# A modulated-convolution kernel whose T1 operand is summed by a DMA in place instead of by GpSimd, with a second G buffer and T0/T4 made one turn sooner

## The chip, the cores and the metric

The kernel runs on one core of a Trainium2 chip. A core has five engines with a queue of instructions each: PE (TensorE, matrix products; PEld is its weight load), DVE (VectorE), ACT (ScalarE), POOL (GpSimd) and SP (SyncE, which here only issues DMAs). An engine takes its instructions strictly in the order of the program and waits on semaphores. The metric is the device time of one execution in microseconds; lower is better.

## The reference

The input x has 128 images of 64 channels and 1024 positions in float32. Each image goes through four 1-D convolution layers of three taps, whose weights are modulated by a style vector of its own, and the result is added to x:

```python
s = style @ mw.T + mb
weight = SCALE * w * s[:, None, :, None]
demod = lax.rsqrt(jnp.sum(weight * weight, axis=(2, 3)) + EPS)
weight = weight * demod[:, :, None, None]
# 'same':       conv, K=3
# 'upsample':   transposed conv with stride 2, then a blur of 4 taps
# 'downsample': blur of 4 taps, then conv with stride 2
# layers: same, upsample, same, downsample
x = x + layers(x)
```

No layer has a nonlinearity, so the four layers of one image are one linear filter along the position axis.

## The kernel before, in words

The kernel uses that linearity. For each group of four images it builds the weights of one combined filter from the four layers (the chain: scale3, stage1, stage2, stage3), and then applies that filter to x. The filter has nine taps. They are applied by a fast-convolution scheme (three by three taps): x is laid out in three planes (position modulo 3), five combinations T0 to T4 of these planes are formed, each is multiplied with its own combination of weights (the five products m = 0 to 4, each three taps), and sums of the products give the three output planes. There are 32 groups q of four images. Two images lie in the two halves of the 128 partitions and two side by side, so that every product is made of matmuls of 64 by 64 weights and 340 positions.

On the way to T0 to T4 stands G, an intermediate of three planes for each of two image pairs: in_g01 writes its planes 0 and 1 and in_g2 its plane 2, all from X, the loaded input. From G come T1 = plane 2 + plane 1 (in1), T2 = plane 2 - plane 1 (in2), and T0 and T4 together (in04). T3 comes from X (in3).

The order is written out by hand: the program is not rescheduled, and each engine's queue holds its instructions in the order in which the Python code issues them. After five opening turns, turn_of(q) runs for q = 4 to 28, and a written-out end follows. In one turn the stages of several groups are mixed: n = q + 1, c = q + 2, s = q + 4. The turn contains the last products of q (conv2, conv4, conv0), the first of n (conv3, conv1), stage2 and stage3 of the weights of c, and stage1 of s. `entry` is true for q = 4 alone.

The places that the change and the prediction's steps touch:

- POOL in a turn: r_sums (L638, two sums of R, the weights after stage2; they are read by the last of the seven groups of matmuls of stage3_b, L621), in2 (L781), a sum of S (L484), in1 (L776).
- DVE in a turn: sum2 (L712 into Y, read by conv4), a difference (L862), six weight combinations (combine_a, combine_b), in04 (L790), share_sums (L501), in_g2, side work that differs from turn to turn (SIDE), two sums of S (L481), in_g01, sum1 (L712 into y, after conv1), in3 (L761), and in turn 13 two instructions of LATE.
- PE in a turn: stage2 (L506), conv2 (L803), stage3_b (L621), conv4 (L803 into Y), stage3_a, conv3, stage1_a (L428), conv0, stage1_b, share, conv1.
- A helper records many instructions under one line: L712 is sum_of, L399 scaled_copy, L803 product.

G has one buffer before, the T tiles have two each, X has two.

Of the kernel before, what the change touches and what calls it, by code (L numbers as in the profile page):

```python
# [48 lines left out]
F32 = mybir.dt.float32  # L49
AF = mybir.ActivationFunctionType  # L50
ALU = mybir.AluOpType
# [12 lines left out]
def kernel(  # L64
# [10 lines left out]
    NP, P, NXC = x.shape  # L75
    B = 2 * NP
    NQ = B // 4
# [5 lines left out]
    nc_v, nc_a, nc_g = nc.vector, nc.scalar, nc.gpsimd  # L83
# [3 lines left out]
    const = ctx.enter_context(tc.tile_pool(name="const", bufs=1))  # L87
# [4 lines left out]
    wf_pool = ctx.enter_context(tc.tile_pool(name="wf_pool", bufs=3))  # L92
    tpool = ctx.enter_context(tc.tile_pool(name="tpool", bufs=2))
    mpool = ctx.enter_context(tc.tile_pool(name="mpool", bufs=1))
    gpool = ctx.enter_context(tc.tile_pool(name="gpool", bufs=1))
    opool = ctx.enter_context(tc.tile_pool(name="opool", bufs=2))
    ps_conv = ctx.enter_context(tc.tile_pool(name="ps_conv", bufs=2, space=PSUM))
    ps_w = ctx.enter_context(tc.tile_pool(name="ps_w", bufs=1, space=PSUM))
# [39 lines left out]
    PL = NXC // 3  # L138
# [27 lines left out]
    def unit(pool, name):  # L166

        if pool is ps_w:
            return [pool.tile([P, 512], F32, tag=f"u{r}", name=f"{name}_{r}") for r in range(2)]
        t = pool.tile([P, 2, 512], F32, tag="u", name=name)  # L170
        return [t[:, r, :] for r in range(2)]


    NB = 340
# [266 lines left out]
    def flat(t):  # L441
        return t.rearrange("c a o -> c (a o)")
# [92 lines left out]
    def stage2_rest(q):  # L535

        ps = shared_ps.pop(q)
        block = lambda i, n=1: [b[:, i * C : (i + n) * C] for b in ps]
        apart = [b[:, : 4 * C].rearrange("c (a b o) -> c a b o", a=2, b=2)[:, :, 0] for b in ps]
        plan = (  # L540
            (apart, E[:, 0], slice(1, 4, 2)),
            (block(1), Ed[:, 0], slice(2, 3)),
            (block(2), Ed[:, 1], slice(1, 2)),
            (block(3), E[:, 2], slice(3, 4)),
            (block(3), Ed[:, 2], slice(2, 3)),
            (block(4), Ed[:, 3], slice(1, 2)),
            (block(4), E[:, 4], slice(3, 4)),
            (block(5, 2), E[:, 8], slice(2, 4)),
            (block(5), E[:, 6], slice(3, 4)),
            (block(1, 2), E[:, 1], slice(4, 6)),  # L550
            (block(2), E[:, 3], slice(4, 5)),
            (block(3), Ed[:, 4], slice(5, 6)),
            (block(4), Ed[:, 5], slice(4, 5)),
            (block(5), E[:, 7], slice(5, 6)),
        )
        for n, (dst, weight, slots) in enumerate(plan):
            chain_matmul(dst, weight, chain[q], slots, n == len(plan) - 1)
        return ps

    def stage2(q, pool=None, engs=(nc_a, nc_a), between=None):  # L560
        if q in shared_ps:
            ps = stage2_rest(q)
        else:
            ps = opened.pop(q, None)
            taps = range(9) if ps is None else range(3, 9)
            ps = stage2_taps(q, taps, ps or unit(pool or ps_w, f"psR{q}"))
        if between:
# [168 lines left out]
    Ts = {}  # L736
    Gs = {}
# [5 lines left out]
    def plane(buf, i, pairs=BOTH_PAIRS):  # L743

        at = PL * (2 - i) if i < 3 else PL * 2 + 1
        return buf[:, pairs, at : at + NJ]
# [16 lines left out]
    def in_g01(q, pairs=BOTH_PAIRS):  # L763
        if q < NQ:
            X, g = g_tile(q)
            sum_of(g[:, pairs, PL:], X[:, pairs, : 2 * PL], 0.5, X[:, pairs, PL:], ALU.subtract)

    def in_g2(q, pairs=BOTH_PAIRS):
        if q < NQ:
            X, g = g_tile(q)  # L770
            sum_of(plane(g, 2, pairs), plane(X, 3, pairs), 0.5, plane(X, 2, pairs), ALU.subtract)

    def in1(q, eng):
        if q < NQ:
            t, g = t_tile(q, "T12"), Gs[q]
            eng.tensor_add(t[:, :, 0, :NJ], plane(g, 2), plane(g, 1))  # L776

    def in2(q, eng):
        if q < NQ:
            t, g = t_tile(q, "T12"), Gs[q]  # L780
            eng.tensor_sub(t[:, :, 1, :NJ], plane(g, 2), plane(g, 1))  # L781

    def in04(q, pairs=BOTH_PAIRS):
        if q < NQ:
            t, g = t_tile(q, "T04"), Gs[q]
            a, b = g[:, pairs, :NJ], g[:, pairs, 2 * PL : 2 * PL + NJ]
            both = lambda v, step: bass.AP(
                v.tensor, v.offset, [*(list(d) for d in v.ap[:-1]), [step, 2], [1, NJ]]
            )
            nc_v.tensor_sub(t[:, pairs, :, :NJ], both(a, PL), both(b, 1))  # L790

    def product(q, m, ps, groups=range(K), alone=False):

        W, H_ = Wq[q]
        tag, i = SLOT[m]
        for g in groups:
            for s, rows in enumerate(HALF):
                for c, cols in enumerate(HALF):
                    if m in (0, 4):
                        w = W[rows, tap(m // 2, g), c, :]  # L800
                    else:
                        w = H_[rows, m - 1, g, c, :]
                    nc.tensor.matmul(  # L803
                        ps[s][cols, :NB],
                        w,
                        Ts[q, tag][rows, c, i, g : g + NB],
                        start=(g == 0 and (m == 3 or alone)),
                        stop=(g == K - 1),
                        skip_group_check=True,
                    )  # L810
# [36 lines left out]
    def sum1(q):  # L847

        y1w[q] = m_tile("y1", q, 2)
        for s, a in parts(q):  # L850
            sum_of(y1w[q][:, s], a, 2.0, m3c[q][:, s])
# [35 lines left out]
            os[q][:, s, planes].rearrange("c i j -> c (i j)"),  # L887
        )


    raw = const.tile([P, 512], F32, name="raw")

    WIDE = 6
    ends_ps = {}
# [94 lines left out]
    g1 = const.tile([P, 6, C], F32, name="g1")  # L989

    Ye = [const.tile([P, HB, 8], F32, name=f"Ye{s}") for s in range(2)]
    Ue = [const.tile([P, HB, 11], F32, name=f"Ue{s}") for s in range(2)]
    Ve = [const.tile([P, HB, 12], F32, name=f"Ve{s}") for s in range(2)]
    Oe = const.tile([P, B, 3], F32, name="Oe")
# [295 lines left out]
    def small(q):  # L1290
        l, bs = SMALL[q]
        dst = high(bs.stop - bs.start)
        src = c0f if l == 0 else cc[l - 1]
        for cols in HALF:
            nc.tensor.matmul(
                dst[cols], wsum[T, l, :], src[T, bs], start=False, stop=True, skip_group_check=True
            )
# [66 lines left out]
    def side(work, q):  # L1364
        work.get(q, lambda: None)()
# [117 lines left out]
    def turn_of(q):  # L1483
        n, c, s = q + 1, q + 2, q + 4
        entry = q == FIRST
        stage2(c)
        if entry:
            sum2(q)
            conv4(q)
            combine_a(n)  # L1490
            r_sums(c, nc_v)
        else:
            conv2(q)
            r_sums(c, nc_g)
            sum2(q)
            in2(n, nc_g)
        side(TABLES, q)
        for i in range(3):
            load(c + 1, slice(i, i + 1))
        stage3_b(c, open_a(n))  # L1500
        if entry:
            conv0(q, 0, 1)
        else:
            combine_a(n)
            conv4(q)
        stage3_a(c)
        combine_b(n)
        conv3(n)
        if entry:
            copy_m3(n)  # L1510
            stage1_a(s)
        outputs(q, 2)
        if not entry:
            if s < NQ:
                stage1_a(s)
            copy_m3(n)
        in04(n)
        if sharing(q):
            share_sums(c + 1)
        in_g2(c)  # L1520
        side(SIDE, q)
        if q in SMALL:
            l, bs = SMALL[q]
            nc_v.memset(high(bs.stop - bs.start), 0.0)
        conv0(q, *((2,) if entry else range(K)))
        if entry:
            conv1(n, 0, 1)
        outputs(q, 1)
        if s < NQ:
            stage1_b(s)  # L1530
        in_g01(c)
        if sharing(q):
            share(c + 1, banks(q))
            share_copy(c + 1)
        outputs(q, 0)
        if q in SLOTS:
            matmuls, width, rest = SLOTS[q]
            slot(matmuls, width, Y_banks)
            rest()
        if s == NQ:  # L1540
            slot(ends3, 3, unit(ps_w, "psE"), 3)
            rest3()
        conv1(n, *((2,) if entry else range(K)))
        if q in SMALL:
            small(q)
        sum1(n)
        in3(c)
        side(LATE, q)
        if s == NQ:
            in04(c)  # L1550
        in1(c, nc_g)
        if s + 1 < NQ:
            scale3(s + 1)

# [3 lines left out]
        turn_of(q)  # L1558

    q, n, c = NQ - 3, NQ - 2, NQ - 1  # L1560
    stage2(c)
    conv2(q)
    in2(n, nc_g)
    stage3(c, 0)
    sum2(q, (0,))
    combine_a(n)
# [26 lines left out]
    q, n = NQ - 2, NQ - 1  # L1593
# [128 lines left out]
```

## Time and profile before

| | us |
|---|---|
| median of 3 runs | 476.29 (475.52 to 476.63) |
| span of the profiled execution, first to last instruction | 475.5 |
| PE busy | 469.7 |
| DVE busy | 417.3 |
| ACT busy | 312.0 |
| POOL busy | 165.8 |
| one steady turn (201.44 to 215.28) | 13.84 |

For the profiled execution the profile gives the span and no separate time; the lowest of the three runs, 475.52, is the same as this span to the last digit shown, so nothing that can be seen lies around it. The granted TensorE clock is 0.998 over the span.

The profile is to be read as follows. PE's busy time is that of pipelined matmuls, and one row of a group of matmuls overlaps the next by a little, so the distance from one start to the next is the better measure. A float32 matmul of the program shows as two records in the trace (one product of 12 matmuls is x24). "Idle before" is the time that an engine had nothing to run ahead of an instruction, with what released it.

### The profile page before, as it was taken

How to read it: one execution, taken by the hardware profiler on the slowest of the kernel's cores; microseconds unless marked ns; L12 is line 12 of the kernel's file. 1: busy time of each engine (PE TensorE's matmuls, PEld its weight loads, DVE VectorE, ACT ScalarE, POOL GpSimd, SP SyncE). 2: the span in 40 equal slices, each digit the busy share in tenths (PEclk: the TensorE clock that was granted, in tenths of full speed). 3: DMA queues.
4: the chain of work that ended last, by engine and by line, in shares of the span. 5: the costliest groups of instructions: out<-in, count | busy, mean ns of one | idle time of the engine just before them, and what ended most of it. 6: DMA issues, size and time to landing. Idle time of an engine off the chain costs nothing.

```text
span 475.5 us, 26771 instructions
## 1 busy us (share of the span) xinstructions
PE 469.7 (99%) x11932; PEld 349.5 (74%) x11932; DVE 417.3 (88%) x694; ACT 312.0 (66%) x711; POOL 165.8 (35%) x200
## 2 busy tenths in 40 slices
PE   9999999999999999999999999999999999999996
PEld 6987788777678876677776677766788787876653
DVE  3889998879989998899979899979998999999896
ACT  4565657577766676766667666667666777766464
POOL 3634033664444342233432233422333423243200
PEclk9999999999999999999999999999999999999999
DMA  5237456535445554345544454543555544455225
GB/s 176 71 115 224 150 151 180 152 113 177 139 145 166 166 166 136 123 150 169 163 150 126 130 168 152 178 124 121 152 164 169 164 145 147 148 152 161 80 91 193
DMA packets 52707, 70.71 MB, mean 149 GB/s; under 512 B 6000, under 2 KB 50672, under 8 KB 52592
## 3 DMA queue, kind: packets, MB, share of 16 engines
q1 hardware_dynamic: 52368, 68.78, 46.3%
q8 instruction: 93, 1.52, 1.4%
q10 hardware_dynamic: 224, 0.22, 0.1%
q14 instruction: 22, 0.18, 0.1%
HBM read 35.36 MB, written 33.62 MB: 145 GB/s over the span
## 4 chain that ended last, share of the span: by engine, by line
PE 99%; DVE 0%; ACT 0%; issue 0%
PE psA L803 47%; PE Y L803 12%; PE psR L506 9%; PE psW L621 7%; PE psA L621 7%; PE psS L428 6%; PE psR L589 5%; PE psA L506 2%; PE Y L1044 2%; PE Y L183 1%; PE Y L379 1%; PE psM L220 0%; PE psE L1044 0%; PE Y L255 0%; DVE o L882 0%; PE psM L255 0%
## 5 line engine op out<-in xcount | busy, mean ns | idle before, releaser
L803 PE MATMUL psA<-T,H 64*64 64x340 f32 x2304 | 185.9, 446 | 0.0
L803 PEld LDWEIGHTS psA<-T,H 64*64 64x64 f32 x2304 | 90.7, 133 | 46.9 <-issue 2.5
L712 DVE SCALAR_TENSOR_TENSOR G<-X 128x1376 f32<-128x1376 f32 (+2 forms) x65 | 78.0, 1206 | 0.2
L776 POOL TENSOR_TENSOR T<-G 128x684 f32<-128x684 f32 x28 | 46.3, 1652 | 73.7 <-DVE G L712 73.7
L484 POOL TENSOR_TENSOR S<-S 128x128 f32<-128x128 f32 x28 | 21.6, 772 | 139.7 <-ACT S L399 139.6
L399 ACT ACTIVATE R<-psR,tC 128x448 f32<-128x448 f32 x63 | 36.6, 631 | 43.6 <-PE psR L506 25.8
L803 PE MATMUL psA<-T,Wf 64*64 64x340 f32 x768 | 63.7, 446 | 0.0
L803 PE MATMUL Y<-T,Wf 64*64 64x340 f32 x768 | 62.4, 451 | 0.0
L712 DVE SCALAR_TENSOR_TENSOR Y<-m,psA 128x340 f32<-128x340 f32 x62 | 32.0, 516 | 28.2 <-PE psA L803 26.9
L399 ACT ACTIVATE psW<-psA 128x128 f32<-128x128 f32 x100 | 19.3, 268 | 49.1 <-PE psA L621 45.0
L790 DVE TENSOR_TENSOR T<-G 128x1368 f32<-128x1368 f32 (+1 forms) x33 | 50.8, 1541 | 0.0
L399 ACT ACTIVATE Wf<-psW,t 128x256 f32<-128x256 f32 (+2 forms) x76 | 32.7, 480 | 26.7 <-PE psW L621 26.4
L761 DVE TENSOR_TENSOR T<-X 128x684 f32<-128x684 f32 x32 | 47.7, 1492 | 0.0
L506 PE MATMUL psR<-S,E 64*64 64x64 f32 (+1 forms) x1472 | 46.8, 237 | 0.0
L781 POOL TENSOR_TENSOR T<-G 128x684 f32<-128x684 f32 x28 | 46.5, 1660 | 0.0
L428 PEld LDWEIGHTS psS<-wd,w2n 64*64 64x64 f32 x1120 | 35.1, 133 | 12.9 <-issue 0.3
L506 PEld LDWEIGHTS psR<-S,E 64*64 64x64 f32 x1472 | 39.5, 134 | 4.9 <-ACT psR L529 0.2
L803 PEld LDWEIGHTS Y<-T,Wf 64*64 64x64 f32 x768 | 30.3, 132 | 16.8
L803 PEld LDWEIGHTS psA<-T,Wf 64*64 64x64 f32 x768 | 29.8, 133 | 14.5
L880 ACT ACTIVATE o<-psA,tb,td 128x340 f32<-128x340 f32 x63 | 37.1, 648 | 5.0 <-PE psA L803 2.8
L880 ACT ACTIVATE o<-y,tb,td 128x340 f32<-128x340 f32 x62 | 38.5, 678 | 0.0
L880 ACT ACTIVATE o<-Y,tb,td 128x340 f32<-128x340 f32 x62 | 36.1, 639 | 2.8 <-PE Y L803 2.0
(180 smaller groups left out, 840.4 us busy)
## 6 DMA issues: line engine op xcount, KB each, us to landing
out<-o SPq DMA_DIRECT2D x191, 170.0 KB, 2.6
X<-in_x SPq DMA_DIRECT2D x150, 172.0 KB, 3.4
X<-in_x SPq DMA_DIRECT2D x14, 516.0 KB, 5.0
par<-in_params SPq DMA_DIRECT2D x3, 192.0 KB, 3.8
Xe<-in_x_ends SPq DMA_DIRECT2D x1, 512.0 KB, 4.5
out<-Oe SPq DMA_DIRECT2D x2, 96.0 KB, 2.1
out<-o ACTq DMA_DIRECT2D x1, 170.0 KB, 2.8
par<-in_params SPq DMA_DIRECT2D x1, 160.0 KB, 2.7
```

Source lines behind the costliest of these rows:

```text
L399: nc_a.activation(dst, src, AF.Copy, scale=f)
L428: nc.tensor.matmul(ps[r][cols, at * C : (at + n) * C], weight[rows], wd[c if r == 0 else 1 - c][rows, taps], start=first, stop=last, skip_ ...
L506: nc.tensor.matmul(dst[r][cols], weight[rows], st[c if r == 0 else 1 - c][rows, slots, :], start=False, stop=last, skip_group_check=True,)
L589: nc.tensor.matmul(ps[r][cols, lo * C : (lo + m) * C], E[rows, e + 2, :], src[rows, a, :], start=(n == 0), stop=(n == 8), skip_group_check ...
L621: nc.tensor.matmul(dst[r][cols], weight[rows], t[rows, c, slots, :], start=first, stop=last, skip_group_check=True,)
L712: nc_v.scalar_tensor_tensor(out, x, f, y, op0=ALU.mult, op1=op)
L761: nc_v.tensor_sub(t[:, pairs, 0, :NJ], plane(X, 3, pairs), plane(X, 1, pairs))
L776: eng.tensor_add(t[:, :, 0, :NJ], plane(g, 2), plane(g, 1))
L781: eng.tensor_sub(t[:, :, 1, :NJ], plane(g, 2), plane(g, 1))
L790: nc_v.tensor_sub(t[:, pairs, :, :NJ], both(a, PL), both(b, 1))
L803: nc.tensor.matmul(ps[s][cols, :NB], w, Ts[q, tag][rows, c, i, g : g + NB], start=(g == 0 and (m == 3 or alone)), stop=(g == K - 1), skip_ ...
L880: nc_a.activation(dst, src, AF.Identity, bias=add, scale=d3)
```

## The change

T1 is no longer a tile of its own in the steady turns. A DMA issued from POOL's queue adds G's plane 1 onto G's plane 2 in place (in1_dma), and the product m = 1 reads its moving operand from there. Since this overwrites plane 2, T2, T0 and T4 of the same group must be made before: in2 moves from the start of the turn of q = n - 1 to the turn before that, ahead of sum1 in the code, and in04 to the end of that turn, behind in3. Since G now lives until conv1 has read it, G has two buffers. in_g01 follows in_g2 directly, ahead of the side work and of the two sums of S. The scratch tile raw, used in the opening, takes over the place of Ye[0]. The opening turns keep in1 and in2 as they were; the entry turn q = 4 does in04 both for n and for c.

```diff
-    gpool = ctx.enter_context(tc.tile_pool(name="gpool", bufs=1))
+    gpool = ctx.enter_context(tc.tile_pool(name="gpool", bufs=2))
...
+    def in1_dma(q):
+
+        g = Gs[q]
+        nc_g.dma_start(plane(g, 2), plane(g, 1), accum_op=ALU.add)
+        first_of[q] = g[:, :, :PL]
...
     def product(q, m, ps, groups=range(K), alone=False):
...
+        if m == 1 and q in first_of:
+            src = first_of[q]
+        else:
+            src = Ts[q, tag][:, :, i]
...
-                        Ts[q, tag][rows, c, i, g : g + NB],
+                        src[rows, c, g : g + NB],
...
-    raw = const.tile([P, 512], F32, name="raw")
...
+    raw = Ye[0].rearrange("c b e -> c (b e)")
...
     def turn_of(q):
         n, c, s = q + 1, q + 2, q + 4
         entry = q == FIRST
+        if not entry:
+            in1_dma(n)
         stage2(c)
...
             conv2(q)
             r_sums(c, nc_g)
             sum2(q)
-            in2(n, nc_g)
...
-        in04(n)
+        if entry:
+            in04(n)
         if sharing(q):
             share_sums(c + 1)
         in_g2(c)
+        in_g01(c)
         side(SIDE, q)
...
             stage1_b(s)
-        in_g01(c)
...
+        in2(c, nc_g)
         sum1(n)
         in3(c)
         side(LATE, q)
-        if s == NQ:
-            in04(c)
-        in1(c, nc_g)
+        in04(c)
...
     q, n, c = NQ - 3, NQ - 2, NQ - 1
+    in1_dma(n)
     stage2(c)
     conv2(q)
-    in2(n, nc_g)
```

Where instructions stand in a queue, from the built programs. In the names, the number behind a letter is the group q and the one behind the underscore a buffer; what stands in brackets are the queues whose semaphores the instruction waits for.

POOL's queue before, from r_sums of group 14 to the sum of S of group 17 (L638 is r_sums, L781 in2, L776 in1):

```order
L638 TENSOR_TENSOR R14_3858<-R14_3858 128x2x128 [waits Activation_49]
L781 TENSOR_TENSOR T12_13_3796<-G13_3729 128x2x342
L484 TENSOR_TENSOR S16_3991<-S16_3991 128x2x64 [waits Activation_49]
L776 TENSOR_TENSOR T12_14_4066<-G14_3999 128x2x342 [waits DVE_49,PE_49,Pool_49]
L638 TENSOR_TENSOR R15_4128<-R15_4128 128x2x128 [waits Activation_49]
L781 TENSOR_TENSOR T12_14_4066<-G14_3999 128x2x342
L484 TENSOR_TENSOR S17_4261<-S17_4261 128x2x64 [waits Activation_49]
```

And now (L789 is in2, L781 the DMA of in1_dma):

```order
L638 TENSOR_TENSOR R14_3860<-R14_3860 128x2x128 [waits Activation_49]
L484 TENSOR_TENSOR S16_3992<-S16_3992 128x2x64 [waits Activation_49]
L789 TENSOR_TENSOR T12_14_4061<-G14_3998 128x2x342 [waits DVE_49,PE_49]
L781 DMA G14_3998<-G14_3998 128x2x342 [waits DMASW6_49,DVE_49,Pool_49]
L638 TENSOR_TENSOR R15_4130<-R15_4130 128x2x128 [waits Activation_49]
L484 TENSOR_TENSOR S17_4262<-S17_4262 128x2x64 [waits Activation_49]
```

The sum L776 is gone, in2 stands where it stood, and the DMA, which waits for DVE (in04) and for in2, stands directly ahead of r_sums.

DVE's queue before, from the sums of S of group 15 to sum2 of group 12 (L712 into G is in_g01, L761 in3, L712 into Y sum2):

```order
L481 SCALAR_TENSOR_TENSOR S15_3721<-psS15_1_3708,tB_132,S15_3721 128x128 [waits PE_49,Activation_49]
L712 SCALAR_TENSOR_TENSOR G13_3729<-X1_106 128x2x688 [waits DMAHW2_49,DMAHW1_49]
L712 SCALAR_TENSOR_TENSOR y1_12_3792<-psA12_3614,m3_12_3724 128x680 [waits PE_49,Activation_49]
L761 TENSOR_TENSOR T3_13_3794<-X1_106 128x2x342
L712 SCALAR_TENSOR_TENSOR Y_119<-m3_12_3724,psA12_3614 128x340 [waits PE_49]
```

And now (L798 is in04):

```order
L712 SCALAR_TENSOR_TENSOR G13_3728<-X1_106 128x2x688 [waits DMAHW2_49,DMAHW1_49]
L1077 TENSOR_TENSOR Ye0_159<-Ye0_159,c0_155 128x64x6
L481 SCALAR_TENSOR_TENSOR S15_3722<-psS15_0_3708,tB_132,S15_3722 128x128 [waits PE_49,Activation_49]
L481 SCALAR_TENSOR_TENSOR S15_3722<-psS15_1_3709,tB_132,S15_3722 128x128 [waits PE_49,Activation_49]
L712 SCALAR_TENSOR_TENSOR y1_12_3793<-psA12_3615,m3_12_3725 128x680 [waits PE_49,Activation_49]
L761 TENSOR_TENSOR T3_13_3795<-X1_106 128x2x342
L798 TENSOR_TENSOR T04_13_3797<-G13_3728 128x4x342 [waits DVE_49]
L712 SCALAR_TENSOR_TENSOR Y_119<-m3_12_3725,psA12_3615 128x340 [waits PE_49]
```

in_g01 has moved ahead of the side work and the sums of S, and in04 from behind the weight combinations to a place between in3 and sum2.

PE's queue now, where stage3_b of group 15 ends and conv4 begins:

```order
L621 MATMUL psA14_4155<-R15_4130,par_97 64x64 x4
L621 MATMUL psA14_4155<-R15_4130,w0s0_150 64x64 x8
L621 MATMUL psA14_4155<-R15_4130,par_97 64x128 [waits Pool_49]
L621 MATMUL psA14_4155<-R15_4130,par_97 64x128 x3
L815 MATMUL Y_119<-T04_13_3797,Wf13_3616 64x340 [waits DVE_49]
```

The order on PE is what it was; the third row is the one that waits for r_sums.

More of the change, by code (lines that the diff above doesn't have):

```diff
@@ L776, in in1 @@
             eng.tensor_add(t[:, :, 0, :NJ], plane(g, 2), plane(g, 1))
+    def in1_dma(q):
+        g = Gs[q]
+        nc_g.dma_start(plane(g, 2), plane(g, 1), accum_op=ALU.add)
+        first_of[q] = g[:, :, :PL]
+    first_of = {}
     def in2(q, eng):
```

## The prediction

> **What bounds the kernel now.** I read the page's busy table first, then the stages, the waits, and last the timeline of one turn. The page (engine, busy time, share of the span, instructions; then a group of instructions with its idle time; then the one DMA queue with real traffic):
>
> ```profile
> PE 469.7 (99%) x11932; PEld 349.5 (74%) x11932; DVE 417.3 (88%) x694; ACT 312.0 (66%) x711; POOL 165.8 (35%) x200
> L776 POOL TENSOR_TENSOR T<-G 128x684 f32<-128x684 f32 x28 | 46.3, 1652 | 73.7 <-DVE G L712 73.7
> q1 hardware_dynamic: 52368, 68.78, 46.3%
> ```
>
> The span is 475.5 us and PE is busy for 469.7 of them: not more than 5.8 us can be gained anywhere while the matmuls stay as they are. POOL works 35% of the time, and in front of L776, the sum that the change takes off POOL, it sat idle for 73.7 us. Two successive steady turns as stages (length, then busy time of each engine), and the waits of the steady part:
>
> ```profile
> 201.44:215.28 13.84, 13.84 (x392) 9.79 (x388) 12.73 (x20) 9.79 (x24) 4.81 (x4) 1.00 0.49 155
> 215.28:229.12 13.84, 13.84 (x392) 9.79 (x388) 12.69 (x21) 9.68 (x24) 4.81 (x4) 1.00 0.50 157
> 345.93:360.19 14.26, 14.06 (x395) 12.15 (x391) 13.27 (x20) 10.00 (x24) 4.46 (x4) 1.00 0.49 152
> ```
> ```profile
> POOL T L776 <- DVE G L712: 60.0, 22, 3.3
> POOL R L638 <- ACT R L399: 35.1, 23, 3.9
> DVE Y L712 <- PE psA L803: 23.9, 22, 1.9
> ```
>
> A turn is 13.84 us of unbroken PE at full clock; one turn of the others is 14.26. The other engines wait for PE, never the reverse for long. So the change cannot win much; it can only be free, or make PE wait. Whether it does is decided at the start of a turn. The timeline there (start, length, engine, line, shape, and in brackets the idle time before):
>
> ```profile
> 210.03 1.58 DVE L790 TENSOR_TENSOR T<-G 128x1368 f32<-128x1368 f32 x1
> 211.53 0.42 DVE L501 TENSOR_TENSOR S<-S 128x256 f32<-128x256 f32 x1
> 211.86 0.87 DVE L712 SCALAR_TENSOR_TENSOR G<-X 128x684 f32<-128x684 f32 x1
> 212.64 0.81 DVE L1066 TENSOR_TENSOR Ye<-Ye,c 128x384 f32<-128x384 f32 x1
> 213.38 0.60 DVE L481 SCALAR_TENSOR_TENSOR S<-psS,tB,S 128x128 f32<-128x128 f32 x2
> 213.90 1.58 DVE L712 SCALAR_TENSOR_TENSOR G<-X 128x1376 f32<-128x1376 f32 x1
> 215.42 0.87 DVE L712 SCALAR_TENSOR_TENSOR y<-psA,m 128x680 f32<-128x680 f32 x1
> 216.21 1.81 DVE L761 TENSOR_TENSOR T<-X 128x684 f32<-128x684 f32 x1
> 219.00 1.07 DVE L712 SCALAR_TENSOR_TENSOR Y<-m,psA 128x340 f32<-128x340 f32 x2 [0.98 <-PE psA L803]
> ```
> ```profile
> 212.21 0.82 POOL L484 TENSOR_TENSOR S<-S 128x128 f32<-128x128 f32 x1 [5.16 <-ACT S L399]
> 215.64 1.65 POOL L776 TENSOR_TENSOR T<-G 128x684 f32<-128x684 f32 x1 [2.61 <-DVE G L712]
> 218.56 0.72 POOL L638 TENSOR_TENSOR R<-R 128x256 f32<-128x256 f32 x1 [1.27 <-ACT R L399]
> 219.25 1.65 POOL L781 TENSOR_TENSOR T<-G 128x684 f32<-128x684 f32 x1
> ```
> ```profile
> 213.38 1.90 PE L803 MATMUL psA<-T,H 64*64 64x340 f32 x24
> 217.03 1.90 PE L803 MATMUL psA<-T,H 64*64 64x340 f32 x24
> 219.86 0.40 PE L621 MATMUL psA<-R,par 64*64 64x128 f32 x8
> 220.12 1.95 PE L803 MATMUL Y<-T,Wf 64*64 64x340 f32 x24
> 221.88 0.40 PE L621 MATMUL psW<-R,wsq 64*64 64x128 f32 x8
> 227.22 1.90 PE L803 MATMUL psA<-T,H 64*64 64x340 f32 x24
> ```
>
> PE ends conv1 at 215.28 (213.38 + 1.90) and conv2 at 218.93 (217.03 + 1.90). At 219.86 stands the last group of stage3_b, the only one that reads what r_sums (POOL L638) writes; r_sums ends at 219.28. This pair has 0.58 us to spare, and it is what the change touches.
>
> **The change part by part.** PE keeps its instructions and shapes: 0. The second buffer of G, the smaller raw, and T1's new address add no instruction: 0.
>
> POOL loses 24 sums of 1.65 us. They were hidden by POOL's idle time (2.61 us ahead of this one), so that alone is worth 0. The difference (in2) moves ahead of the turn's end. It needs in_g01, which now follows in_g2: DVE comes free of the weight combinations at 210.03, then share_sums, in_g2 and in_g01 take 0.33, 0.78 and 1.52 (starts 211.53 to 211.86 to 212.64, and 213.90 to 215.42), to 212.66. POOL's L484 (0.82 us, which needs ACT at 212.21) ends by 213.5 even if it waits for in_g01, and in2 by 215.2. The conv2 that reads it is that of the next turn but one, at 217.03 + 13.84, more than 15 us later: 0.
>
> DVE's in3 gets shorter. It took 1.81 us beside POOL's in1; nearer the end of the kernel, with POOL at rest, it took less:
>
> ```profile
> 454.29 0.87 DVE L712 SCALAR_TENSOR_TENSOR G<-X 128x684 f32<-128x684 f32 x1
> 455.07 0.87 DVE L761 TENSOR_TENSOR T<-X 128x684 f32<-128x684 f32 x1
> ```
>
> With in2 over by 215.2, in3 should take 0.87, and 0.94 us of DVE time a turn come free. DVE waits for PE next, so this is worth 0 by itself; but it sets when in04 ends. The Trainium skill, SBUF — State Buffer, section Who interferes with whom, says that a DVE instruction with two SBUF inputs and a POOL instruction that reads SBUF exclude each other for the whole instruction; 1.81 against 0.87 agrees (in3 ended 0.73 us after in1 did). Were the 1.81 in3's own, the wait worked out below would be 0.94 us longer in each turn, 22.6 us more.
>
> in04 moves from 210.03 to behind in3. The sum before it (L712, y) can start 0.07 us after conv1, as L712 at 219.00 does after conv2: 215.35. With steps of 0.79 (215.42 to 216.21) and 0.78, in3 starts at 216.14 and in04 at 216.92; in04 ends at 218.50. The next DVE instruction waits for conv2 until 219.00, so DVE is not late.
>
> The DMA is new. POOL issues it after in04 of the same image, at 218.50 + 0.07 = 218.57, and r_sums stands directly behind it in POOL's queue. r_sums would have started at 218.56. So whatever time POOL needs to issue the DMA, call it t, lands on r_sums whole: it starts at 218.57 + t. Of the spare 0.58 us, 0.07 go by until PE sees that r_sums is done (as between conv2's end and 219.00), and 0.01 by the later start. PE waits t - 0.5 us. Nothing gives it back: the wait delays conv1, conv1 delays in3 and in04, and these set the next issue. It is paid in all 24 turns that have r_sums on POOL:
>
> ```profile
> L638 POOL TENSOR_TENSOR R<-R x24: 724/730/897, 105.2 to 432.8; 128x256 f32<-128x256 f32 x24
> L146 SPq DMA_DIRECT2D X<-in_x x164: 327/423/2069, 3.6 to 433.7; - x164
> DMA to landing us min/median/max: 2.3/3.5/6.6
> ```
>
> No row shows a DMA issued by POOL, so t is bounded by SP's issues (ns, minimum, median, maximum). Lower end: 0.33 us, SP's shortest, no wait. Upper end: 2.07, SP's longest: 1.57 x 24 = 37.7 us. I take three times SP's median, 1.27 us. A load of one plane reads 128 runs and writes 128; the accumulation has two runs per partition, reads source and destination and writes, 768 against 256. That it also lies between SP's 0.42 and the 1.65 of the POOL instruction that handles the same planes makes it plausible. It is an estimate. The wait is then 0.77 us, and 24 x 0.77 = 18.5 us.
>
> The Trainium skill, DMA: Bandwidth & Descriptors, section Latency and other measured facts, puts a POOL-issued DMA's first byte at about 1 us and an SP-issued one's at 0.6. By that ratio an estimate of t would be 0.70, the cost 24 x 0.2 = 5 us, and the total 481, inside the range of the forecast; no run here shows it.
>
> The data path: the DMA adds 128 x 2 x 342 x 4 bytes = 0.35 MB, read twice and written once, 1.05 MB per turn, to 155 GB/s x 13.84 us = 2.15 MB at a DMA share of 0.49: at most 0.73, no bound. conv1 of that image starts at 227.22, 8.6 us after the issue. Loads on SP land in 3.5 us, at most 6.6: 0.
>
> Smaller terms, with a row of the chain of waits and two of DVE:
>
> ```profile
> 217.21 1.72 PE psA L803 x24
> ```
> ```profile
> 226.48 1.00 DVE L1016 SCALAR_TENSOR_TENSOR g<-par,g 128x192 f32<-128x192 f32 x2
> 227.41 0.60 DVE L481 SCALAR_TENSOR_TENSOR S<-psS,tB,S 128x128 f32<-128x128 f32 x2
> ```
>
> conv4 takes from 220.12 to 221.88, 1.76 us, for what takes 1.72 elsewhere: it waits a little for sum2 on DVE. That goes by under the new wait: -0.04 x 24 = -1.0. In turn 13 (LATE) two instructions like those at 226.48 come between in3 and in04: 0.9 us, once. Turn 4 does in04 twice, 1.58 us more of DVE against the 0.94 that in3 gives back; what is left over, once, is less than the rounding here: 0. SP issues the same DMAs in the same order, and its loads wait for in3, which ends earlier: 0. In the last turns no r_sums stands behind the DMA. There in04 and conv1 are these:
>
> ```profile
> 446.24 1.57 DVE L790 TENSOR_TENSOR T<-G 128x1368 f32<-128x1368 f32 x1
> 453.98 1.89 PE L803 MATMUL psA<-T,H 64*64 64x340 f32 x24
> ```
>
> With the shorter in3, in04 ends at 446.9, and 7 us are left to land the data, more than SP's longest 6.6: 0.
>
> Sum against the profiled execution: 475.5 + 18.5 - 1.0 + 0.9 = 493.9. The median of the runs, 476.29, stands 0.8 above this execution, so the forecast is 494.5.
>
> **The rivals.** A, the forecast: POOL's issue holds r_sums and PE waits at L621. For it: the queue order and a spare of 0.58. Against it: t is not measured.
>
> B, not slower: POOL issues as quickly as SP, t at most 0.5 us (SP's median is 0.42). Then r_sums ends in time, nothing else is near the path, and PE stays full. The time is 476.2, or up to 1.2 us less if the shorter in3 also removes waits such as the 0.4 us of the turn of 14.26. It decides at t = 0.5.
>
> C, the data is late: conv1 waits for the DMA itself. The way round is then landing time L, conv1 1.90, then 3.3 to the next issue (215.28 to 218.57): L + 5.2 against 13.84 + 0.77, so it decides at L = 9.4. At L = 12 it costs 2.6 us in 24 turns on top of A, 556. SP's longest landing of 6.6 speaks against it; that the sum is done in the transfer leaves it open.
>
> D, DVE is late: if in3 still meets a POOL instruction, in04 ends at 219.44, not 218.50; the sum for conv4 is 0.4 late and so is r_sums by 0.94. With t = 0.5 this alone is 24 x 0.94 = 22.6 us, 499; it decides where in3 meets POOL at all.
>
> **How the numbers follow.** Chances: A 0.72, B 0.14, C 0.08, D 0.06. The predicted time is A's, 494.5. A's own range is 478 to 513 (t from 0.57 to 2.07). The whole range, 476 to 512, takes in the slower half of B and leaves out C, A's far end and B's gains. 0.2% of 476.3, some 1 us, is about what the runs can tell from no change. Faster by more than that: a part of B, 0.05. Within it: the rest of B, 0.09. Slower: A, C and D, 0.86.
>
> **What would show it.** In the profile after, r_sums should start later against the ACT instruction that feeds it, with the DMA issue just ahead of it on POOL, and PE should idle in front of the last L621 group of stage3_b, released by POOL, 24 times with 0.2 to 1.5 us each; turns should be 13.84 plus that. in3 should take 0.87 us, which tests the first step, and in04 should end just before the DMA is issued, which tests the second. If PE is idle ahead of L815 instead, released by a DMA, C holds. If turns stay at 13.84, the issue is cheap and B holds. The forecast is wrong if t is under 0.5 us, or if POOL starts r_sums without finishing the issue.

## The result, and the profile after

The changed kernel takes 503.68 us (median of 4 runs, 503.20 to 504.99) against 476.01 for the kernel before, run beside it: a ratio of 1.0581 [1.0563, 1.0599]. The profiled execution took 503.20 us with a span of 501.4, so 1.8 us lie outside the span; in all executions here that have both numbers it is 1.7 to 2.2. The profiled execution of the kernel before, with its span of 475.5 us, was therefore one of some 477 us, and not the lowest of the three as the section on the time before took it; that is why the span grew by 25.9 us and the median by 27.7. The page (engines; the DMA's issue; the matmuls of stage3_b; the new DMA queue), then the waits:

```profile
PE 471.0 (94%) x11932; PEld 339.1 (68%) x11932; DVE 400.5 (80%) x694; ACT 311.0 (62%) x711; POOL 148.3 (30%) x200
L781 POOL DMA_DIRECT2D G<-G x25 | 30.1, 1205 | 127.3 <-issue 119.8
L621 PE MATMUL psA<-R,par 64*64 64x64 f32 (+1 forms) x400 | 18.9, 255 | 24.5 <-POOL R L638 24.5
q0 software_dynamic: 6800, 8.76, 10.6%
```
```profile
PE psA L621 <- POOL R L638: 24.5, 24, 1.7
```

PE's busy time is nearly what it was (471.0 against 469.7). What is new is a wait of PE for r_sums, 24 times, in front of L621. One steady turn on DVE, POOL and PE, from the timeline (start, length, engine, line, shape, idle before):

```profile
222.78 0.86 DVE L761 TENSOR_TENSOR T<-X 128x684 f32<-128x684 f32 x1
223.56 1.58 DVE L798 TENSOR_TENSOR T<-G 128x1368 f32<-128x1368 f32 x1
225.57 1.07 DVE L712 SCALAR_TENSOR_TENSOR Y<-m,psA 128x340 f32<-128x340 f32 x2 [0.44 <-PE psA L815]
```
```profile
225.67 1.19 POOL L781 DMA_DIRECT2D G<-G  x1 [4.82 <-issue]
226.45 1.18 POOL L638 TENSOR_TENSOR R<-R 128x256 f32<-128x256 f32 x1
```
```profile
227.68 0.45 PE L621 MATMUL psA<-R,par 64*64 64x128 f32 x8 [1.07 <-POOL R L638]
```

in04 (L798) ends at 225.14. The DMA's record begins 0.53 us later and lasts 1.19, to 226.86; the last 0.77 us of r_sums's record are its own work, to 227.63, and 0.05 later PE goes on. PE had been idle for 1.07 us. From the start of one sum2 to the next, a steady turn has 15.05 us in place of 13.84: 1.21 us more. Over the 25 turns from turn 4 to turn 28 the starts of sum2 move apart by 28.2 us in all. The opening, up to the first sum2, is 2.4 us shorter in this execution (86.5 us against 88.9), which makes the 25.9. In the other kernels below the opening is 86.9 to 89.3 us. Of the 2.4 us, 2.0 stand ahead of the first sum2 of all (27.9 us against 29.9); why the openings differ is open.

### The profile page after: what moved, and what is told of

Same layout as the page of the kernel before. It is cut to its first block, busy times and chain, and to the rows that moved or that the text cites. A ratio compares the mean times of both kernels' runs of the same rounds, so it can differ in the third digit from the quotient of the medians.

```text
span 501.4 us, 26777 instructions
## 1 busy us (share of the span) xinstructions
PE 471.0 (94%) x11932; PEld 339.1 (68%) x11932; DVE 400.5 (80%) x694; ACT 311.0 (62%) x711; POOL 148.3 (30%) x200
## 4 chain that ended last, share of the span: by engine, by line
PE 61%; issue 24%; POOL 10%; DVE 3%; DMA 1%; ACT 1%; SPq 0%; DVEq 0%; POOLq 0%
PE psA L815 29%; PE Y L815 11%; PE psW L621 7%; POOL G L781 6%; PE psS L428 5%; PE psR L589 4%; POOL R L638 4%; PE psA L621 2%; PE psA L506 2%; DVE T L798 1%; DMA par_s<-in_params_s 1%; PE Y L1055 1%; DVE G L712 1%; DVE T L761 0%; POOL T L789 0%
## 5 line engine op out<-in xcount | busy, mean ns | idle before, releaser
L815 PE MATMUL psA<-T,H 64*64 64x340 f32 x1704 | 137.3, 446 | 0.0
L815 PEld LDWEIGHTS psA<-T,H 64*64 64x64 f32 x1704 | 63.7, 133 | 36.6 <-issue 1.8
L712 DVE SCALAR_TENSOR_TENSOR G<-X 128x1376 f32<-128x1376 f32 (+2 forms) x65 | 76.4, 1212 | 0.0
L781 POOL DMA_DIRECT2D G<-G x25 | 30.1, 1205 | 127.3 <-issue 119.8
L484 POOL TENSOR_TENSOR S<-S 128x128 f32<-128x128 f32 x28 | 12.9, 460 | 161.0 <-ACT S L399 124.6
L712 DVE SCALAR_TENSOR_TENSOR y<-psA,m 128x680 f32<-128x680 f32 x31 | 26.9, 866 | 34.3 <-PE psA L815 31.3
L798 DVE TENSOR_TENSOR T<-G 128x1368 f32<-128x1368 f32 (+1 forms) x33 | 50.9, 1542 | 0.0
L789 POOL TENSOR_TENSOR T<-G 128x684 f32<-128x684 f32 x28 | 46.8, 1671 | 5.5 <-DVE G L712 5.5
L815 PE MATMUL psA<-G,H 64*64 64x340 f32 x600 | 47.5, 446 | 0.0
L506 PE MATMUL psR<-S,E 64*64 64x64 f32 (+1 forms) x1472 | 45.5, 237 | 0.0
L712 DVE SCALAR_TENSOR_TENSOR Y<-m,psA 128x340 f32<-128x340 f32 x62 | 32.0, 516 | 15.7 <-PE psA L815 14.6
L621 PE MATMUL psA<-R,par 64*64 64x64 f32 (+1 forms) x400 | 18.9, 255 | 24.5 <-POOL R L638 24.5
L506 PEld LDWEIGHTS psR<-S,E 64*64 64x64 f32 x1472 | 37.4, 134 | 5.6
L712 DVE SCALAR_TENSOR_TENSOR H<-Wf 128x384 f32<-128x384 f32 x64 | 39.9, 623 | 0.0
```

The lines of the kernel that those rows point to most:

```text
L506: nc.tensor.matmul(dst[r][cols], weight[rows], st[c if r == 0 else 1 - c][rows, slots, :], start=False, stop=last, skip_group_check=True,)
L621: nc.tensor.matmul(dst[r][cols], weight[rows], t[rows, c, slots, :], start=first, stop=last, skip_group_check=True,)
L712: nc_v.scalar_tensor_tensor(out, x, f, y, op0=ALU.mult, op1=op)
L781: nc_g.dma_start(plane(g, 2), plane(g, 1), accum_op=ALU.add)
L815: nc.tensor.matmul(ps[s][cols, :NB], w, src[rows, c, g : g + NB], start=(g == 0 and (m == 3 or alone)), stop=(g == K - 1), skip_group_chec ...
```

## Experiments

All kernels are the changed kernel with the edit shown. Times are medians, and each ratio is to runs of the kernel before made beside it (medians 476.01 to 476.58); "steady" is the commonest distance between two starts of sum2, and the last column the sum of the 25 distances less that of the kernel before.

| kernel | time, us | ratio to before | steady | turn 13 | turn 18 | 25 turns |
|---|---|---|---|---|---|---|
| before | 476.01 | | 13.84 | 13.84 | 13.95 | 0 |
| changed | 503.68 | 1.0581 [1.0563, 1.0599] | 15.05 | 15.19 | 15.05 | +28.2 |
| half the runs | 496.98 | 1.0440 [1.0410, 1.0470] | 14.72 | 14.87 | 15.27 | +20.2 |
| two DMAs | 544.06 | 1.1421 [1.1380, 1.1462] | 15.94 | 17.77 | 17.62 | +64.0 |
| copy on POOL | 492.60 | 1.0352 [1.0325, 1.0378] | 14.59 | 14.60 | 15.22 | +17.2 |
| copy on SP | 478.88 | 1.0050 [1.0032, 1.0069] | 13.84 | 14.78 | 15.30 | +1.9 |
| DMA behind r_sums | 480.23 | 1.0074 [1.0051, 1.0097] | 13.84 | 14.79 | 15.30 | +4.1 |
| r_sums on DVE | 480.21 | 1.0078 [1.0053, 1.0104] | 13.84 | 14.78 | 15.31 | +3.4 |
| POOL sum, no DMA | 483.29 | 1.0138 [1.0115, 1.0161] | 13.84 | 14.77 | 18.03 | +7.2 |
| in04 ahead of sum1 | 484.92 | 1.0177 [1.0152, 1.0203] | 14.2 to 14.3 | 14.44 | 15.30 | +8.3 |
| in_g01 back | 485.38 | 1.0186 [1.0156, 1.0217] | 14.22 | 14.88 | 14.20 | +8.6 |
| side work first | 477.80 | 1.0043 [1.0022, 1.0064] | 13.84 | 14.40 | 13.92 | +1.8 |

### Is it the place in POOL's queue?

Theory: all of the wait is r_sums standing behind the issue. Rivals: late data (C) or a late DVE (D). The first run puts the DMA behind r_sums, the second takes r_sums off POOL.

```diff
-        if not entry:
-            in1_dma(n)
         stage2(c)
...
             r_sums(c, nc_g)
+            in1_dma(n)
```

> The DMA is issued behind r_sums instead of ahead of it; nothing else is changed. Theory (POOL's issue, about 0.5 us from in04's end to its start and 1.19 us of its own, holds r_sums, and PE waits for r_sums): r_sums is in time again, the turn is 13.84 us and the time 476 to 480; some turns may wait for the DMA's data, since the longest landing of the changed kernel, 9.3 us, is more than the 7.4 us that are left before conv1. Rival 1 (the data is late, or the added traffic slows the loads): the data comes later still, 503 or more. Rival 2 (the moved DVE work, in04 ahead of sum2 and in_g01 ahead of the sums of S, is what costs): 503 as before.

```diff
-            r_sums(c, nc_g)
+            r_sums(c, nc_v)
```

> r_sums runs on DVE instead of POOL, so that it is not behind the DMA issue; the DMA stays where it is. Theory: 476 to 478, turns of 13.84 us, since DVE waits there for PE anyway (0.44 us in the changed kernel) and r_sums took 0.46 us on DVE. Rival 1 (data, traffic): 503. Rival 2 (the moved DVE work costs): 503 or more, since DVE gets 0.46 us more just there.

They give 480.23 and 480.21 us, with steady turns of 13.84: the 1.21 us per turn are gone in both. Both totals lie above what was expected, the second by 2 us. The data is in time in nearly all turns although the issue is no earlier. It is late in turns 25 and 27 of the first kernel and in turns 21 and 24 of the second: there conv1 starts 0.14 us behind the landing, the least in any trace, and the turns are 0.29, 0.16, 0.53 and 0.12 us longer. The DVE, ACT and POOL rows of the first kernel (timeline):

```profile
215.41 1.58 DVE L798 TENSOR_TENSOR T<-G 128x1368 f32<-128x1368 f32 x1
215.75 1.16 ACT L399 ACTIVATE R<-psR,tC 128x448 f32<-128x448 f32 x2 [0.93 <-PE psR L506]
216.99 0.73 POOL L638 TENSOR_TENSOR R<-R 128x256 f32<-128x256 f32 x1 [3.61 <-DVE T L798]
217.66 1.18 POOL L781 DMA_DIRECT2D G<-G  x1
```

Two things are to be seen. r_sums reads nothing that in04 (L798) writes, and yet the waits name in04 17 times:

```profile
POOL R L638 <- DVE T L798: 66.0, 17, 6.5
```

It is not in04 that it waited for. ACT's copy of R ends at 216.91 and r_sums starts 0.08 us later. That distance is 0.08 in all 24 turns of this kernel, as in the kernel before, also where in04 was over 0.9 us earlier. in04 only happens to end in the same moment, and the DMA's own wait for in04 is recorded just ahead of r_sums, so the view counts it for r_sums. A real hold of r_sums by in04 can be seen further down, in the kernel with in_g01 back: there r_sums starts under in04, ends 0.59 us behind it and takes 1.48 us in place of 0.73. The Trainium skill, SBUF — State Buffer, section Who interferes with whom, states that a DVE instruction with two SBUF inputs, as in04 is, contends with a POOL instruction that reads SBUF, and those rows agree.

The other thing: the issue follows r_sums without a gap, while behind an idle POOL it begins 0.53 us after in04. The lag has gone by under r_sums: the issue at 217.66 stands 0.67 us after in04's end, and no issue from POOL in any trace stands less than 0.53 after it.

The third run has the same duty as the DMA, but done by POOL as before, directly behind in2, with every other edit of the change kept:

```diff
-        if not entry:
-            in1_dma(n)
...
         in2(c, nc_g)
+        in1(c, nc_g)
         sum1(n)
...
-    in1_dma(n)
     stage2(c)
```

> All of the change but the DMA: T1 is a tile of its own again and is made by POOL's sum, directly behind in2; two G buffers, and in2, in04 and in_g01 where the change puts them. Theory: no issue, so turns of 13.84 us and 475 to 476.5. Rival 2 (the moved DVE work or the second buffer costs): 500 or more. Rival 1 says 476 as the theory does, since there is no transfer.

It takes 483.29 us, not the 475 to 476.5 of the theory, and not the 500 of its rival either. The steady turns are 13.84, so the moved DVE work is free there. The loss sits in single turns, 4.1 us of it in turn 18; see below.

### What makes the issue dear?

A run, in what follows, is an unbroken stretch of 342 values in one partition; the DMA of the changed kernel has 256 of them, 128 partitions by two image pairs.

> The DMA takes only pair 0 of the image: 128 runs per side in place of 256, half the bytes. It leaves out the sum of the other pair, so T1 of pair 1 is G's third plane alone. In the changed kernel the issue holds POOL for 1.19 us and begins 0.53 us after in04; r_sums is behind it and a steady turn is 15.05 us. Theory P (the time is per run): the issue takes 0.6 us, the steady turn 14.45, the total 503.7 - 24 x 0.6 = 489 us. Theory F (a fixed price per DMA, whatever its size): issue 1.19, turn 15.05, total 503 to 504. The 0.53 us ahead of the issue should stay under both.

```diff
-        nc_g.dma_start(plane(g, 2), plane(g, 1), accum_op=ALU.add)
+        nc_g.dma_start(plane(g, 2, PAIR[0]), plane(g, 1, PAIR[0]), accum_op=ALU.add)
```

> The same DMA from POOL as a plain copy, without accumulation. It leaves out the sum: T1 is G's second plane alone. If the price of the issue is that of any DMA that POOL issues: issue 1.19 us, lag 0.53, total 503 to 504 us. If it is the accumulation that is dear: the issue falls towards SP's 0.42, and the total to 503.7 - 24 x 0.77 = 485 us. The landing time, 6.0 us with accumulation, should fall towards the 4 us of the loads, which moves the total by nothing, since conv1 was not waiting.

```diff
-        nc_g.dma_start(plane(g, 2), plane(g, 1), accum_op=ALU.add)
+        nc_g.dma_start(plane(g, 2), plane(g, 1))
```

> The plain copy again, issued on SP in place of POOL; it leaves out the sum as the run before does. If the loss of the changed kernel is the time that POOL spends on the DMA ahead of r_sums, it goes: steady turns of 13.84 us and about 480 us, like the two runs that took r_sums from behind the issue. The rival: SP's queue holds the loads of this turn behind the copy, which waits for in04; the loads then start some 1.5 to 2 us later, and if they are needed by then, turns of 14.2 us and 485 to 490 us, with PE or DVE waiting for the loads in the chain.

```diff
-        nc_g.dma_start(plane(g, 2), plane(g, 1), accum_op=ALU.add)
+        nc.sync.dma_start(plane(g, 2), plane(g, 1))
```

The view of one line gives the issue's shortest, median and longest length (ns), and below it how long the data takes from the issue until it has landed. In this order: the changed kernel, half the runs, the copy on POOL, the copy on SP.

```profile
L781 POOL DMA_DIRECT2D G<-G x25: 1193/1193/1381, 102.9 to 473.3; - x25
DMA to landing us min/median/max: 4.3/6.0/9.3
```
```profile
L781 POOL DMA_DIRECT2D G<-G x25: 867/870/1053, 104.3 to 466.7; - x25
DMA to landing us min/median/max: 2.9/5.2/6.3
```
```profile
L781 POOL DMA_DIRECT2D G<-G x25: 722/724/922, 103.4 to 462.8; - x25
DMA to landing us min/median/max: 2.8/5.5/6.8
```
```profile
L781 SPq DMA_DIRECT2D G<-G x25: 605/606/694, 105.0 to 449.2; - x25
DMA to landing us min/median/max: 2.8/3.0/4.8
```

Half the runs cost 0.87 us, not 0.60 and not 1.19. If the price is linear in the runs, these two lengths make it 0.55 us for any accumulating DMA and 2.5 ns for each of the 256 runs. (Half the runs are also half the bytes; these kernels do not tell the two apart.) Without accumulation the same 256 runs cost 0.72: the sum in the transfer makes up 0.47 of the 1.19. The turn follows to 0.01 us: 15.05 - 14.72 = 0.33 for 1.19 - 0.87 = 0.32, and 15.05 - 14.59 = 0.46 for 0.47. That is the chain in04, issue, r_sums, PE, with nothing beside it. The lag ahead of the issue stays, 0.54 and 0.55 us in these two. Both expected totals for half the runs (489 and 503) were missed, and so were those for the copy (485 and 503); the truth lies between.

The same copy from SP makes no engine wait in a steady turn: 478.88 us, steady turns 13.84. Its issue takes 0.61 us of SP's time and lands in 3.0 us where POOL's took 5.5. The first half of the rival did occur. Here is SP's queue in one turn, first with the DMA behind r_sums on POOL, then with the copy on SP (L897 are stores, L146 the loads of x):

```profile
329.63 5.52 SPq L897 DMA_DIRECT2D out<-o  x6
335.24 4.40 SPq L146 DMA_DIRECT2D X<-in_x  x6
```
```profile
329.87 5.51 SPq L897 DMA_DIRECT2D out<-o  x6
338.02 0.61 SPq L781 DMA_DIRECT2D G<-G  x1
338.68 4.08 SPq L146 DMA_DIRECT2D X<-in_x  x6
```

From the first store to the first load it is 5.61 us in the one and 8.81 in the other: the loads stand behind the copy, which waits for in04, and start 3.2 us later. They are still early enough, so the second half of the rival, turns of 14.2 us, did not follow.

> The same transfer cut into two DMAs of one pair each, both ahead of r_sums; nothing is left out. Theory P: two issues of 0.6 us, the steady turn stays at 15.05 and the total at 503 to 504 us. Theory F: two issues of 1.19 us, the turn grows by 1.19 to 16.24 and the total by 24 x 1.19 = 28.6 to 532 us. If a second lag of 0.53 us stands between the two issues, 24 x 0.53 = 12.7 us come on top under either.

```diff
-        nc_g.dma_start(plane(g, 2), plane(g, 1), accum_op=ALU.add)
+        nc_g.dma_start(plane(g, 2, PAIR[0]), plane(g, 1, PAIR[0]), accum_op=ALU.add)
+        nc_g.dma_start(plane(g, 2, PAIR[1]), plane(g, 1, PAIR[1]), accum_op=ALU.add)
```

The total, 544 us, is near the sum of a fixed price and a second lag (532 + 12.7), but for another reason. The commonest turn is 15.94, only 0.89 longer than with one DMA. The timeline of PE shows the rest; here two turns, each with the wait and then conv4 (L816), which takes 1.90 us elsewhere:

```profile
210.78 0.45 PE L621 MATMUL psA<-R,par 64*64 64x128 f32 x8 [1.95 <-POOL R L638]
211.05 1.90 PE L816 MATMUL Y<-T,Wf 64*64 64x340 f32 x24
...
226.72 0.45 PE L621 MATMUL psA<-R,par 64*64 64x128 f32 x8 [1.95 <-POOL R L638]
226.99 3.03 PE L816 MATMUL Y<-T,Wf 64*64 64x340 f32 x24
```
```profile
227.60:231.01 3.41, 3.41 (x44) 2.18 (x40) 3.34 (x6) 1.31 (x5) 0.00 (x0) 0.50 0.52 93
```

The last row (a view of the busy time in a stretch; after the engines come the granted clock, the DMA share and GB/s) shows the clock at 0.50 for 3.41 us, from within the slow conv4 on. In 23 of the 24 turns the wait is 1.73 to 2.29 us; conv4 ran slow behind 9 of these, and a turn with it has 17.6 us in place of 15.94. Waits of the same 1.95 us stand on both sides. In the changed kernel, with waits of up to 1.72, the clock stays at 1.00 throughout the turns. All nine falls last 3.41 us, at 0.50, and so cost 1.7 us each; and they start whole multiples of 3.413 us apart (5, 15, 30, 35, 60, 94, 99 and 109 of them after the first). So it seems to matter where a wait lies against that grid; no run here moves a wait along it. Of the 38 us that the profiled execution takes more than that with one DMA, 24 x 0.89 = 21 are wait and 9 x 1.7 = 15 are clock; the opening is 2.3 us longer.

The 0.89 is 0.34 more than the 0.55 of the linear price. The rows of POOL and DVE show from where:

```profile
224.40 1.19 POOL L782 DMA_DIRECT2D G<-G  x1
224.97 1.70 POOL L638 TENSOR_TENSOR R<-R 128x256 f32<-128x256 f32 x1
...
225.47 0.63 DVE L712 SCALAR_TENSOR_TENSOR H<-Wf 128x384 f32<-128x384 f32 x1
```

The second issue ends at 225.59, 2.31 us behind in04 in place of 1.72, which is near the linear price. But r_sums ends 1.08 us behind it, not 0.77 as with one DMA. In between DVE has started a weight combination (L712 into H), and r_sums ends 0.56 us behind the end of that instruction, in 22 of the 24 turns. In the other two, where r_sums and this instruction do not meet so, r_sums ends 0.75 us behind the issue. So r_sums, made later by the second DMA, meets a DVE instruction that it does not meet in the changed kernel.

### Where the rest comes from

Without the wait, 2 to 4 us remain against the kernel before (of these, 1.62 in turn 14 of the kernel with the DMA behind r_sums and 0.69 in turn 17 of that with r_sums on DVE, each in that one alone, were not traced). The copy on SP shows it most cleanly: +0.94 us in turn 13, +1.35 in turn 18, and nothing else above 0.15 that is a loss. Turn 18 in that kernel (DVE, POOL, PE; timeline), and the side work L1102 of the kernel before, which is the same instruction as L1113:

```profile
300.28 2.76 DVE L1113 SCALAR_TENSOR_TENSOR Ue<-b1s,Ue 64x64 f32<-64x64 f32 x4
303.07 0.61 DVE L481 SCALAR_TENSOR_TENSOR S<-psS,tB,S 128x128 f32<-128x128 f32 x2
...
300.64 1.69 POOL L789 TENSOR_TENSOR T<-G 128x684 f32<-128x684 f32 x1
...
303.92 0.60 PE L506 MATMUL psR<-S,E 64*64 64x128 f32 x6 [0.98 <-ACT psR L529]
```
```profile
299.06 1.39 DVE L1102 SCALAR_TENSOR_TENSOR Ue<-b1s,Ue 64x64 f32<-64x64 f32 x4
```

The side work doubles, 1.39 to 2.76 us, since in2 now runs on POOL beside it; the sums of S (L481) come late, and ACT's copy of them, and PE waits. With both POOL sums there (the POOL sum without DMA) the same side work takes 4.21 us, PE waits 2.45, and the granted clock from 304 to 308 us is 0.65:

```profile
300.52 4.21 DVE L1113 SCALAR_TENSOR_TENSOR Ue<-b1s,Ue 64x64 f32<-64x64 f32 x4
...
305.62 0.76 PE L506 MATMUL psR<-S,E 64*64 64x128 f32 x6 [2.45 <-ACT psR L529]
```
```profile
304.00:308.00 4.00, 2.38 (x68) 2.38 (x72) 3.95 (x7) 2.61 (x6) 0.33 (x1) 0.65 0.18 59
```

Turn 13 of the copy on SP is the same case (its side work L1027 is L1016 of the kernel before, where it takes 1.00 us):

```profile
226.77 2.35 DVE L1027 SCALAR_TENSOR_TENSOR g<-par,g 128x192 f32<-128x192 f32 x2
227.13 1.78 POOL L789 TENSOR_TENSOR T<-G 128x684 f32<-128x684 f32 x1
...
234.08 1.07 DVE L712 SCALAR_TENSOR_TENSOR Y<-m,psA 128x340 f32<-128x340 f32 x2 [0.71 <-PE psA L815]
```

The sums of S start only at 229.05, and PE waits 0.46 us at L506. The late work of this turn, between in3 and in04, is not the cause: DVE sits idle for 0.71 us ahead of the next sum2.

Two runs move things to test this, both on top of the DMA behind r_sums.

```diff
         in_g2(c)
-        in_g01(c)
         side(SIDE, q)
+        in_g01(c)
...
-        side(LATE, q)
         in04(c)
+        side(LATE, q)
```

> The kernel with the DMA behind r_sums (480.2 us), with the side work of a turn ahead of in_g01 (so that in2, which needs in_g01, cannot run beside it) and the late work of turn 13 behind in04. If it is in2 beside the side work that lengthens these turns, and the late work that delays in04 in turn 13, turn 13 returns from 14.49 to 13.84 and turns 14, 18 and 19 lose 0.5 to 1.5 us each: 476.5 to 478.5 us. The rival: the sums of S are then delayed by in_g01 instead (1.52 us), and the total stays at 479.5 to 481 us.

477.80 us, as the theory said: turn 18 is back at 13.92 (its side work takes 1.12 us), and turn 13 is at 14.40, from 14.79 (not from 14.49, as the expectation has it). This kernel is the best of those with the DMA, and still 0.43% [0.22, 0.64] slower than the kernel before. What is left in turn 13, 0.56, is the late work, which now stands directly ahead of sum2: sum2 starts when it ends, and conv4 on PE waits for sum2:

```profile
234.08 1.95 PE L815 MATMUL Y<-T,Wf 64*64 64x340 f32 x24 [0.40 <-DVE Y L712]
```

The remaining +0.76 in turn 7 and +0.63 in turn 21 were not traced to a cause.

```diff
         in_g2(c)
-        in_g01(c)
         side(SIDE, q)
...
             stage1_b(s)
+        in_g01(c)
```

> The kernel with the DMA behind r_sums (480.2 us), and in_g01 back at its old place behind stage1_b; the difference in2 on POOL then starts later, beside sum1 and in3. If the moved in_g01 and in2 cost what is left against the kernel before (in2 holds side work and the sums of S on DVE in some turns), side turns return to their old lengths (turn 18: 13.84 in place of 15.0) and the total to 476 to 478 us. The rival: in3 now meets in2 and takes 1.81 us again, in04 ends about 0.9 us later, r_sums, which starts only when in04 ends, is late at PE by about 0.4 us in each turn, and the total is 480 + 24 x 0.4 = 490 us.

485.38 us. Turn 18 loses its extra (14.20, the length of its steady turns), but the steady turns have 14.22, 0.38 more. The rival had said 0.4 per turn; its total of 490 was not reached, since turns 10, 14, 15, 19 and 22, which are longer for other reasons, lose nothing. Its rows:

```profile
219.01 1.65 POOL L789 TENSOR_TENSOR T<-G 128x684 f32<-128x684 f32 x1 [2.90 <-DVE G L712]
219.64 1.75 DVE L761 TENSOR_TENSOR T<-X 128x684 f32<-128x684 f32 x1
221.32 1.57 DVE L798 TENSOR_TENSOR T<-G 128x1368 f32<-128x1368 f32 x1
222.00 1.48 POOL L638 TENSOR_TENSOR R<-R 128x256 f32<-128x256 f32 x1 [1.34 <-ACT R L399]
```
```profile
PEld Y L815 <- DVE Y L712: 4.8, 19, 1.5
PEld psA L621 <- POOL R L638: 3.4, 12, 0.9
```

in3 takes 1.75 beside in2, in04 ends late, at 222.89, and r_sums, which started under it at 222.00, ends at 223.48. In the 19 turns in which r_sums starts under in04, it ends 0.58 to 0.59 us behind it. PE's weight load waits for both sum2 and r_sums.

The last run puts in04 ahead of sum1, so that the issue comes earlier:

```diff
         in2(c, nc_g)
+        in04(c)
         sum1(n)
         in3(c)
         side(LATE, q)
-        in04(c)
```

> in04 goes ahead of sum1, into DVE's idle time before conv1's end; the DMA is still directly ahead of r_sums. Theory: the issue can start about 1.5 to 2.5 us earlier and is over before ACT has R ready, so r_sums is in time: 476 to 479. Rival 1 (data, traffic): the data comes earlier by the same, so it says some gain too, but turns would still show waits ahead of conv1. Rival 3 (any POOL instruction next to an issue is slowed, wherever the issue stands): r_sums or in2 stay longer than 0.73 and 1.65 us and the time stays over 485.

It takes 484.92 us, not the 476 to 479 of the theory. r_sums is in time, but the wait has moved:

```profile
289.66 2.20 POOL L789 TENSOR_TENSOR T<-G 128x684 f32<-128x684 f32 x1
...
290.76 2.54 DVE L798 TENSOR_TENSOR T<-G 128x1368 f32<-128x1368 f32 x1
293.22 0.85 DVE L712 SCALAR_TENSOR_TENSOR y<-psA,m 128x680 f32<-128x680 f32 x1
...
294.13 0.80 PE L815 MATMUL psA<-T,H 64*64 64x340 f32 x8 [0.24 <-DVE y L712]
```

in04 now meets in2; they take 2.54 and 2.20 us. sum1 starts only behind it, and conv2 on PE, which overwrites what sum1 reads, waits for sum1.

## Why the prediction was right, and where it was off

**The mechanism: right.** The forecast named the instruction that waits (the last L621 group), the one it waits for (r_sums), the reason (the issue directly ahead of it on POOL) and the count, 24. The waits show the first two and the count, POOL's rows the reason, and two kernels that separate r_sums from the issue lose the wait whole. The forecast of 494.5 us is 9.2 short of 503.7. (Its own terms, 493.9 and 0.8, add up to 494.7.)

**in3 and in04: right.** in3 takes 0.86 us (0.87 predicted) and DVE is idle for 0.44 us ahead of sum2; that in3's 1.81 was POOL's doing is shown by the run with in_g01 back, where in3 takes 1.74 us or more again in most turns.

**"The DMA issue at 218.57", 0.07 us after in04: this step failed.** The 0.07 was taken from a compute instruction that waits. The DMA's record begins 0.53 us after in04. Counted from in04's end, r_sums is free after 0.53 + 1.19 = 1.72 us and has its last 0.77 us of work then; the forecast had 0.07 + 1.27 = 1.34 and 0.72. The sum of these, 2.49 against 2.06, is 0.43 us more per turn; 0.77 + 0.43, less the 0.04 of conv4's own small wait, makes 1.16 where 1.21 was measured. Over 24 turns the step is worth 10 us, which is what the forecast lacked (9.2) and a little more; the shorter opening works the other way.

**t = 1.27: close, 1.19 measured, though not by its reasoning.** The estimate scaled with the reads and writes of the transfer. The runs give 0.72 for the plain copy and 0.47 for the accumulation, and half the runs do not halve it.

**The rule on the first byte (the Trainium skill, DMA: Bandwidth & Descriptors, section Latency and other measured facts; it gave 481): no measure of this price.** POOL's issue against SP's, for the same copy, is 0.72 against 0.61, and the landing 5.5 against 3.0.

**LATE in turn 13: right for the changed kernel.** Predicted 0.9 once; the wait in that turn is 1.72 us in place of 1.07, so 0.65. That the runs without the wait have +0.94 in turn 13 is a coincidence: there it is the side work beside in2.

**in2 and in_g01 at 0: off in turns with side work.** The prediction looked at a steady turn, and there it holds. In turns 13 and 18 they cost 0.94 and 1.35 once the wait for r_sums is gone; in the changed kernel the two do not meet (in turn 18 the side work takes 1.30 us and ends at 313.78, in2 starts at 313.61), and the turn has 15.05 like the others.

**B, not slower:** it needed t of 0.5 at most. With the lag, even the plain copy from POOL has 1.27. **C, the data late:** it was to decide at a landing of 9.4 us. The median is 6.0 and the longest 9.3. In the changed kernel the data lands 1.6 us or more ahead of conv1 in every turn but turn 6, that of the 9.3, where conv1 starts 0.14 us behind the landing. Late data does appear in the two kernels without the wait, four times, at 0.53 us a turn or less. **D, DVE late:** it did not happen in the changed kernel; in the run with in_g01 back it did, at 0.38 us per turn.

## What to carry to other kernels

A DMA moved onto POOL's queue is an instruction of POOL: it has a price of its own and may wait, and whatever stands behind it in the queue pays both. Put it behind the work that others wait for, not ahead; here that was worth 23 us. When POOL and DVE instructions that read SBUF are moved, check in every kind of turn, the rare ones too, which partner they meet next. And when a view of waits names an engine whose result is not read, compare the start with the other inputs before you believe it.

## What the runs showed that had not been expected

- An accumulating DMA of 256 runs holds POOL for 1.19 us, of which a plain copy is 0.72, and when POOL waits for its input there are 0.53 to 0.55 us more between the end of that input and the start of the record. Behind r_sums the lag does not show, since it goes by while r_sums runs.
- The same SBUF-to-SBUF copy lands in 3.0 us from SP and in 5.5 us from POOL.
- With two DMAs PE's granted clock fell after waits of 1.76 to 1.96 us in 9 of 24 turns, and in others, with the same waits, it did not; each fall lasted 3.41 us and cost 1.7. The Trainium skill, TensorE: Matmul & The Clock Gate, section Part 1, puts the idle window behind which the clock halves at about 3.4 us and says that this window runs freely; waits clearly shorter than that did it here, and that the falls stand on one grid of 3.41 us agrees with a free-running window.
